# Softmax subtraction and scaling and the experts' low parts on GpSimd behind the first block, outputs added in three chunks

## The chip, the cores and the metric

The kernel runs on one core of a Trainium2 chip. The metric is the device time of one execution in microseconds; the time before is 1141.91 us, the median of 3 runs (1141.68 to 1142.55).

Engine names follow the profile: PE is TensorE (PEld its weight loads), DVE is VectorE, ACT is ScalarE, POOL is GpSimd, SP is SyncE, whose queue issues the DMAs of this kernel.

## The reference

4096 rows (2 x 2048) of 512 features go through a latent attention and then through a gated expert layer whose weights are quantised to three values. Each branch is normalised on its way in and on its way out and added to the row.

```python
Q = (h @ Wq.T + bq).reshape(b, t, H, HD).transpose(0, 2, 1, 3)      # H=16 heads, HD=32
V = (h @ Wv.T + bv).reshape(b, t, H, HD).transpose(0, 2, 1, 3)
attn_logits = einsum('bhtd,lhd->bhtl', Q, latent) / sqrt(HD)         # L=64 latents
topk_logits, topk_idx = top_k(attn_logits, 4)
weights = softmax(topk_logits)
weighted = einsum('bhtk,bhtkd->bhtd', weights, selected latents)
attn = (weighted + V).transpose(0, 2, 1, 3).reshape(b, t, d) @ Wo.T + bo
...
wu, wg, wd = ternary_quant(W_up), ternary_quant(W_gate), ternary_quant(W_down)
hidden = silu(x @ wu.T) * (x @ wg.T)                                 # 2048 wide
ffn = hidden @ wd.T
...
x = x + layernorm(attn(layernorm(x)))
x = x + layernorm(ffn(layernorm(x)))
```

## The kernel before, in words

The rows are cut into 8 blocks b of 512 rows, each of four tiles t of 128 rows. The expert layer of a block runs in 16 steps e, one for each 128 of the 2048 hidden features. While the experts of block b run, the attention of block b + 1 is spread over the same steps, and some of block b + 2's input normalisation. The order of all instructions on every engine and queue is the order in which the program writes them; each engine works through its own queue in that order, and a waiting instruction holds what is behind it. The synchronisation itself is made by the tile framework.

One step of the experts (the loop over e at the end of the kernel): eight matmuls into the up product `pu`; `tanh` on ScalarE; `silu` on VectorE (L728); eight matmuls into the gate product `pg`; `gate` on VectorE (L733), which makes `h`; `high` on ScalarE (L744), which rounds `h` to fp32r as `hi`; `low` (L749), which makes `lo = h - hi`; and in the next step `down` (L759), where TensorE multiplies `hi` and `lo` (as weights) with a piece of the down matrix into the accumulators `acc` of the four tiles. The down projection of step e - 1 comes behind the gate matmuls of step e; that of step 15 is in step 0 of the next block. [...]

Between these pieces the step has four slots, called by `do(k)`: slot 3 ahead of `tanh`, slot 0 behind it, slot 1 behind the gate matmuls, and slot 2 behind `down`. The function `pieces` says which piece of the next block's attention is put in which slot of which step. For the attention of a block, i runs from 0 to 7 over pairs of heads:

- `q(c)`: query matmuls (L353) and the copy `qT` with bias on ScalarE (L358); `l(c)`: logits (L367) and their copy `w` on ScalarE, for i = 2c and 2c + 1
- `m(i)`: the 8 largest of each 64 (L385); `r(i)`: eight match_replace (L393) that mark the four taken, then `w - best` (L395) and `top - best` (L397), all on VectorE
- `e(i)`: the exponentials of `top` (L402) and of `w` (L403) on ScalarE
- `n(i)`: sum and reciprocal of the four, the masking of `w` (L410), and its scaling by the reciprocal (L413), on VectorE
- `z(i)`: a transpose within blocks on VectorE (L420), a DMA of the result to DRAM (`dz`, L425) and four DMAs back (`wT`, L428), which complete the transpose
- `v(c)` and `y(c)`: value matmuls (L440), and on top of them the matmuls of the weights `wT(2c)` and `wT(2c+1)` with the latents (L457); `attnT` is the copy on ScalarE
- `o(t)`, `o_bias`, `o_rstd`, `o_apply_scalar`: output projection, bias and normalisation; `o_apply_scalar` adds the row on GpSimd (L502); then `f_stats` to `f_split`, the normalisation and transposed hi/lo halves that the experts of the next block read

Block 0 has an attention of its own ahead of all, in the order of a written list (`FIRST_STEPS`), and block 1's attention, a `FirstAttention` as well, runs in block 0's steps. In the steps of blocks 1 to 6 the attentions of blocks 2 to 7 run; block 7 has experts alone. `pieces` puts m(i) in slot 0 of step 1 + i (slot 1 for i = 0), r(i) in slot 2 of step 1 + i, n(i) and z(i) in slot 1 of step 2 + i, e(i) in slot 3 of step 2 + i; q(2) and q(3) in slot 0 of steps 3 and 5; and for c = 0 and 1 v(c), y(c) and l(c + 2) in slot 0 of step 4 + 2c, for c = 2 and 3 v(c) and y(c) in slot 1 of that step. o(t) are in step 10, the additions of L502 in step 11.

The experts' output of block b is finished in the steps of block b + 1: the last `down`, statistics and reciprocal root in step 0, and `y_out` for the four tiles in step 1, which normalises on VectorE (L276), adds the row on GpSimd (L810) and stores it (L812, on SP). In block 7 the four are spread over steps 1 and 2.

Of the kernel before, what the change touches and what calls it, by code (L numbers as in the profile page):

```python
# [10 lines left out]
F32 = mybir.dt.float32  # L11
# [3 lines left out]
ALU = mybir.AluOpType  # L15
AX = mybir.AxisListType

P = 128
H = 16
HD = 32  # L20
L = 64
# [37 lines left out]
def latent_attention_ternary_glu(  # L59
# [15 lines left out]
    nc = tc.nc  # L75
# [6 lines left out]
    NB = NT // TB  # L82
    G = 2 * TT
# [39 lines left out]
    for n, i in RAW_ORDER:  # L123
        raw[n, i] = wpool.tile([P, CH], F32, tag="chunk", name=f"raw_{n}_{i}", bufs=6 * DC)
# [21 lines left out]
    def load_up(n, src, pieces):  # L146
        for i in pieces:
            k, h = halves[i]
            nc.sync.dma_start(
                out=raw[n, i], in_=src[k * P : (k + 1) * P, h * CH : (h + 1) * CH]  # L150
            )
# [88 lines left out]
    class Norm:  # L240
        def __init__(self, name):
            self.name = name
            self.mv = small.tile([P, TT, 2], F32, tag="mv", name=f"mv_{name}")
            self.rs = small.tile([P, TT], F32, tag="rs", name=f"rs_{name}")
            self.nm = None
# [34 lines left out]
    def row(name):  # L280
        return work.tile([P, D], F32, tag="row", name=name, bufs=4)
# [9 lines left out]
    class Attention:  # L291
        def __init__(self, b):
            self.b = b
            self.hT = None
            self.attnT = None
            self.norm_a = Norm(f"a{b}")
            self.norm_o = Norm(f"o{b}")
            self.norm_f = Norm(f"f{b}")
            self.rows = {}
            self.qT, self.w, self.top, self.m8, self.left, self.wT, self.pv = ({} for _ in range(7))  # L300
            self.po = {}
            self.far = {}
# [85 lines left out]
        def r(self, i):  # L388
            w, m8 = self.w[i], self.m8.pop(i)
            left = work.tile([P, G, L], F32, tag="left", name=f"left_{self.b}_{i}", bufs=2)  # L390
            self.left[i] = left
            for g in range(G):
                nc.vector.match_replace(left[:, g, :], m8[:, g, :], w[:, g, :], TAKEN)  # L393
            best = m8[:, :, 0:1]
            nc.vector.tensor_tensor(w, w, best.to_broadcast([P, G, L]), ALU.subtract)  # L395
            self.top[i] = small.tile([P, G, K_TOP], F32, tag="top", name=f"top_{self.b}_{i}", bufs=2)
            nc.vector.tensor_tensor(  # L397
                self.top[i], m8[:, :, 0:K_TOP], best.to_broadcast([P, G, K_TOP]), ALU.subtract
            )
# [5 lines left out]
        def n(self, i):  # L405
            w = self.w[i]
            ri = small.tile([P, G], F32, tag="ri", name=f"ri_{self.b}_{i}", bufs=2)
            nc.vector.tensor_reduce(ri, self.top.pop(i), AX.X, ALU.add)
            nc.vector.reciprocal(ri, ri)
            nc.vector.scalar_tensor_tensor(  # L410
                w, self.left.pop(i), TAKEN, w, ALU.is_equal, ALU.mult
            )
            nc.vector.tensor_tensor(  # L413
                w, w, ri.rearrange("p (g o) -> p g o", o=1).to_broadcast([P, G, L]), ALU.mult
            )

# [123 lines left out]
    class FirstAttention(Attention):  # L540
# [111 lines left out]
        def b_low(self):  # L652
            low = row("bias_low")
            nc.vector.tensor_tensor(low, bo_sb, self.bias.bitcast(F32), ALU.subtract)
            nc.vector.tensor_scalar(low, low, ident[:, 1:2], 0.0, ALU.mult, ALU.add)
            nc.vector.scalar_tensor_tensor(
                self.bias, self.bias.bitcast(F32), ident[:, 0:1], low, ALU.mult, ALU.add
            )
# [43 lines left out]
    class Experts:  # L702
# [43 lines left out]

        def low(self, e):
            lo = self.part("lo", e)
            nc.vector.tensor_tensor(lo, self.h.pop(e), self.hid[e][0].bitcast(F32), ALU.subtract)  # L749
            self.hid[e].append(lo)  # L750

        def down(self, e, tiles=range(TT), last=True):
# [46 lines left out]
            r = self.b * TB + t * P  # L799
            nc.sync.dma_start(out=out[r : r + P, part], in_=x[:, part])  # L800

        def y_out(self, t, engine=nc.gpsimd):
            x = x_tiles[self.b][t]
            if self.b == NB - 2:
                y = self.y[t]
                self.norm.apply(y, y, t)
            else:
                y = row(f"y_{self.b}_{t}")
                self.norm.apply(y, self.acc[t], t)
            engine.tensor_tensor(x, x, y, ALU.add)  # L810
            r = self.b * TB + t * P
            nc.sync.dma_start(out=out[r : r + P, :], in_=x)  # L812

# [3 lines left out]
    A = FirstAttention(0)  # L817
# [119 lines left out]
    def pieces(A, after):  # L937

        at = {(e, k): [] for e in range(EC) for k in range(4)}

        def put(e, k, f, *args):
            at[e, k].append(lambda: f(*args))

        if A.b > 1:
            put(0, 2, A.q, 0)
            put(1, 1, A.q, 1)
            put(3, 0, A.q, 2)
            put(5, 0, A.q, 3)
        put(1, 0, A.l, 0)
        put(2, 0, A.l, 1)  # L950
        for i in range(8):
            put(1 + i, 0 if i else 1, A.m, i)
            put(1 + i, 2, A.r, i)
            put(2 + i, 3, A.e, i)
            put(2 + i, 1, A.n, i)
            put(2 + i, 1, A.z, i)
        for c in range(2):
            if A.b > 1:
                put(4 + 2 * c, 0, A.v, c, gate_psum)
                put(4 + 2 * c, 0, A.y, c)  # L960
            put(4 + 2 * c, 0, A.l, c + 2)
            if A.b == 1:

                put(4 + 2 * c, 2 - c, A.v, c)
                put(4 + 2 * c, 2 - c, A.y, c)
        for c in range(2, DC):
            put(4 + 2 * c, 1, A.v, c)
            put(4 + 2 * c, 1, A.y, c)

        if after is not None and after.b == 2:  # L970
            for t in range(TT):
                put(10, 2, after.a_stats, t)
            put(10, 2, after.a_rstd, 0, TT)
        elif after is not None:
            put(9, 2, after.a_stats, 0)
            put(9, 2, after.a_stats, 1)
            put(10, 0, after.a_stats, 2)
            put(10, 0, after.a_stats, 3)
            put(10, 0, after.a_rstd, 0, TT)
            for t in range(TT):  # L980
                put(10, 1, after.a_apply, t)
            for t in range(TT):
                put(10, 2, after.a_blocks, t)
        put(10, 2, A.o, 0, range(DC), gate_psum)
        put(10, 2, A.o_bias, 0)
        for t in range(1, TT):
            if after is not None and after.b == 2:
                for i in (t - 1,) if t < 3 else (2, 3):
                    put(10, 2, after.a_apply, i)
                    put(10, 2, after.a_blocks, i)  # L990
            put(10, 2, A.o, t)
            put(10, 2, A.o_bias, t)
        put(10, 2, A.o_rstd, 0, 2)
        put(10, 2, A.o_rstd, 2, 4)
        for t in range(TT):
            put(11, t // 2, A.norm_o.shift, t)
            put(11, t // 2, A.o_apply_scalar, t)
        put(11, 2, A.f_stats, 0)
        put(11, 2, A.f_stats, 1)
        put(11, 2, A.f_rstd, 0, 2)  # L1000
        put(12, 0, A.f_stats, 2)
        put(12, 0, A.f_stats, 3)
        put(12, 0, A.f_rstd, 2, 4)
        for t in range(TT):
            put(12, 1 + t // 2, A.norm_f.shift, t)
            put(12, 1 + t // 2, A.f_apply_scalar, t)
        put(12, 2, A.f_blocks, 0)
        put(12, 2, A.f_blocks, 1)
        put(13, 0, A.f_blocks, 2)
        put(13, 0, A.f_blocks, 3)  # L1010
        put(13, 0, A.f_load, 0)
        put(13, 1, A.f_load, 1)
        for t in range(TT):
            put(14 + t // 2, 2 - t // 2, A.f_split, t)
        if after is not None:
            put(15, 2, after.a_load)
        return at

    prev = None
    for b in range(NB):  # L1020
        if b > 0:
            A, nxt = nxt, after
        after = None
        F = Experts(b, A.split())
        at = {}
        for e in range(EC):
# [25 lines left out]
            F.silu(e)  # L1052
            if e == 1 and 0 < b < NB - 1:
                for t in range(TT):
                    prev.y_out(t)
            F.up("g", e)
            do(1)
            F.gate(e)
            F.high(e)
            if e == EC - 1 and b == NB - 1:  # L1060

                nc.scalar.activation(columns[:, 11:12], columns[:, 10:11], AF.Sqrt)
# [12 lines left out]
            if e == 0 and prev is not None:  # L1075
# [2 lines left out]
                        prev.y_copy(t)  # L1078
                    prev.y_stats(t)
                prev.y_rstd(0, TT)  # L1080
            if e > 0 or b < NB - 1:
                F.low(e)
            if b == NB - 1 and e in (1, 2):
                prev.y_out(2 * e - 2)
                prev.y_out(2 * e - 1)
        prev = F


# [77 lines left out]
```

## Time and profile before

| what | us |
|---|---|
| median of 3 runs | 1141.91 |
| span of the profiled execution | 1140.3 |
| one block of 1 to 6 (831.02 / 6) | 138.5 |
| TensorE busy in such a block | 138.35 |
| VectorE busy in block 2 | 104.73 |
| GpSimd busy in block 2 | 17.50 |
| ScalarE busy in block 2 | 43.45 |

The profile gives the execution's span from its first to its last instruction; the runs' time has some 1.6 us more. In the profile's lines an instruction is named by its engine, its line in the code, its operation and out<-in with the program's tile names; x8 stands for eight instructions. A row of costly groups ends with their busy time and the mean nanoseconds of one, and, behind a second bar, the idle time of the engine just ahead of them with what ended it. A line of the order of time begins with its start and its duration in us from the span's start. A row of a stretch has its length, then busy time and (x instructions) of PE, PEld, DVE, ACT and POOL, the granted clock, and the share and rate of the DMAs. SPq is the queue that issues DMAs: the duration there is that of the issue, and the page's last part gives the time from issue to landing.

### The profile page before, as it was taken

The numbers are of one execution on the slowest core, as the hardware profiler recorded it, in microseconds if no ns is written. First come the engines' busy times: TensorE is split into PE (matmuls) and PEld (weight loads), VectorE is DVE, ScalarE is ACT, GpSimd is POOL, SyncE is SP. The second block draws the span as 40 slices with busy tenths as digits, with TensorE's granted clock in tenths as the row PEclk, the third lists the DMA queues.
The fourth block names the chain that finished last, engine by engine and source line by source line (L and its number), as shares of the span: only waits on it lengthen the run. The fifth ranks groups of instructions, "written<-read, shape, count | busy, mean of one in ns | idle before, by whom it ended". The sixth has DMA issues, their size and how long they took to land.

```text
span 1140.3 us, 14487 instructions
## 1 busy us (share of the span) xinstructions
PE 1127.9 (99%) x4602; PEld 771.9 (68%) x4602; DVE 836.3 (73%) x2952; ACT 411.9 (36%) x714; POOL 163.5 (14%) x203
## 2 busy tenths in 40 slices
PE   9999999999999999999999999999999999999997
PEld 5547666767667675776657766586675866758886
DVE  6978968687866887678877778678786787847435
ACT  4985642332233332333214333153321433224223
POOL 1057003110032000320002200022001120021200
PEclk9999999999999999999999999999999999999999
DMA  9800221432213322222222222232321412102000
GB/s 350 305 0 20 74 93 38 111 120 84 82 52 98 102 86 81 72 77 93 93 74 75 83 93 95 63 99 66 112 75 56 111 65 93 61 5 74 37 1 37
DMA packets 98428, 97.16 MB, mean 85 GB/s; under 512 B 8368, under 2 KB 70832, under 8 KB 98352
## 3 DMA queue, kind: packets, MB, share of 16 engines
q1 hardware_dynamic: 98352, 96.24, 26.8%
q8 instruction: 36, 0.59, 0.2%
q14 instruction: 40, 0.33, 0.1%
HBM read 59.51 MB, written 36.70 MB: 84 GB/s over the span
## 4 chain that ended last, share of the span: by engine, by line
PE 89%; DVE 5%; DMA 4%; ACT 1%; issue 0%; SPq 0%; ACTq 0%; DVEq 0%
PE pg L716 20%; PE pu L716 19%; PE acc L759 19%; PE po L468 8%; PE pv L440 8%; PE pq L353 7%; PE pv L457 2%; PE pl L367 2%; DMA raw_d<-in_wdT 1%; DVE left L393 1%; DMA raw_g<-in_wgT 1%; DMA wv<-in_wvT 1%; DVE m L385 1%; DMA raw_u<-in_wuT 1%; PE pq L577 1%; DMA hT<-far_a 1%
## 5 line engine op out<-in xcount | busy, mean ns | idle before, releaser
L716 PE MATMUL pg<-hT_f,tern_g 128*128 128x512 f32 x512 | 207.8, 406 | 0.0
L716 PE MATMUL pu<-hT_f,tern_u 128*128 128x512 f32 x512 | 204.8, 401 | 0.0
L759 PE MATMUL acc<-tern_d,hi 128*128 128x512 f32 x512 | 203.6, 398 | 0.0
L759 PE MATMUL acc<-tern_d,lo 128*128 128x512 f32 x512 | 200.0, 391 | 1.0 <-DVE lo L749 0.9
L716 PE MATMUL pg<-lT_f,tern_g 128*128 128x512 f32 x512 | 199.8, 390 | 0.0
L716 PE MATMUL pu<-lT_f,tern_u 128*128 128x512 f32 x512 | 199.1, 390 | 0.0
L725 ACT ACTIVATE h<-pu,columns 128x512 f32<-128x512 f32 x128 | 87.1, 680 | 202.8 <-PE pu L716 202.8
L728 DVE SCALAR_TENSOR_TENSOR h<-h,pu 128x512 f32<-128x512 f32 x128 | 85.9, 671 | 93.5 <-ACT h L725 93.5
L744 ACT CAST hi<-h 128x512 fp32r<-128x512 f32 x128 | 79.1, 618 | 199.2 <-DVE h L733 199.1
L733 DVE TENSOR_TENSOR h<-h,pg 128x512 f32<-128x512 f32 x128 | 86.5, 675 | 63.4 <-PE pg L716 62.3
L759 PEld LDWEIGHTS acc<-tern_d,hi 128*128 128x128 f32 x512 | 96.2, 188 | 32.8 <-issue 13.6
L716 PEld LDWEIGHTS pg<-hT_f,tern_g 128*128 128x128 f32 x512 | 96.2, 188 | 25.3 <-issue 1.4
L716 PEld LDWEIGHTS pu<-hT_f,tern_u 128*128 128x128 f32 x512 | 96.1, 188 | 25.1 <-issue 3.1
L759 PEld LDWEIGHTS acc<-tern_d,lo 128*128 128x128 f32 x512 | 96.2, 188 | 22.9 <-DVE lo L749 2.2
L716 PEld LDWEIGHTS pu<-lT_f,tern_u 128*128 128x128 f32 x512 | 96.2, 188 | 22.5 <-issue 3.1
L716 PEld LDWEIGHTS pg<-lT_f,tern_g 128*128 128x128 f32 x512 | 96.3, 188 | 21.5 <-issue 2.9
L749 DVE TENSOR_TENSOR lo<-h,hi 128x512 fp32r<-128x512 f32 x128 | 89.9, 702 | 23.1 <-ACT hi L744 23.1
L440 PE MATMUL pv<-hT,wv 128*128 128x512 f32 x224 | 100.8, 593 | 0.3 <-ACT w L375 0.3
L393 DVE MATCH_REPLACE8 left<-m,w 128x64 f32<-128x64 f32 x512 | 100.3, 209 | 0.0
L468 PE MATMUL po<-wo,attnT 128*128 128x512 f32 x224 | 97.3, 592 | 0.0
L353 PE MATMUL pq<-hT,wq 128*128 128x512 f32 x192 | 86.7, 595 | 0.9 <-DMA hT<-far_a 0.6
L468 PEld LDWEIGHTS po<-wo,attnT 128*128 128x128 f32 x224 | 42.6, 190 | 50.7 <-issue 48.3
(140 smaller groups left out, 1312.0 us busy)
## 6 DMA issues: line engine op xcount, KB each, us to landing
dz<-z SPq DMA_DIRECT2D x56, 256.0 KB, 2.0
wT<-dz SPq DMA_DIRECT2D x224, 64.0 KB, 1.9
x<-in_x SPq DMA_DIRECT2D x32, 256.0 KB, 3.7
out_x<-x SPq DMA_DIRECT2D x32, 256.0 KB, 2.0
far_f<-zf SPq DMA_DIRECT2D x28, 256.0 KB, 2.8
hw<-far_f SPq DMA_DIRECT2D x56, 128.0 KB, 3.5
xa<-in_x SPq DMA_DIRECT2D x6, 1024.0 KB, 5.3
far_a<-za SPq DMA_DIRECT2D x24, 256.0 KB, 2.9
```

The source lines that it names most:

```text
L353: nc.tensor.matmul(pq, lhsT=wq[:, k, c * P : (c + 1) * P], rhs=self.taken(k), start=(k == 0), stop=(k == DC - 1),)
L367: nc.tensor.matmul(pls[pr][:, t * P : (t + 1) * P], lhsT=qT[rows, t * P : (t + 1) * P], rhs=lk[rows, c, :], start=True, stop=True, tile_po ...
L393: nc.vector.match_replace(left[:, g, :], m8[:, g, :], w[:, g, :], TAKEN)
L440: nc.tensor.matmul(self.pv[c], lhsT=wv[:, k, c * P : (c + 1) * P], rhs=self.ordered(k), start=(k == 0), stop=False,)
L468: nc.tensor.matmul(self.po[t], lhsT=self.attnT[:, c, t * P : (t + 1) * P], rhs=wo[:, c, :], start=(c == 0), stop=(c == DC - 1),)
L716: nc.tensor.matmul(p, lhsT=tern[n, 2 * k + e // 8][:, (e % 8) * P : (e % 8 + 1) * P], rhs=self.parts[i][:, k], start=(k, i) == pairs[0], s ...
L725: nc.scalar.activation(self.h[e], self.pu[e], AF.Tanh, scale=half_u[0])
L728: nc.vector.scalar_tensor_tensor(self.h[e], self.h[e], 1.0, self.pu.pop(e), ALU.add, ALU.mult)
L733: nc.vector.tensor_tensor(self.h[e], self.h[e], self.pg.pop(e), ALU.mult)
L744: nc.scalar.copy(hi, self.h[e])
L749: nc.vector.tensor_tensor(lo, self.h.pop(e), self.hid[e][0].bitcast(F32), ALU.subtract)
L759: nc.tensor.matmul(self.acc[t], lhsT=part[:, t * P : (t + 1) * P], rhs=wd, start=(e == 0 and i == 0), stop=(e == EC - 1 and i == 1),)
```

## The change

In blocks above 1 the attention's subtraction of the largest value (L395) and its scaling (L413) go to GpSimd (`aside`). In the steps of blocks 1 to 6 the experts' `low` goes to GpSimd, and its place in the program from behind slot 2 to directly behind `high`; in the first and the last block it stays on VectorE. For the attentions that run in blocks 1 to 6, e(i) goes from slot 3 to slot 0 and is put first of the three lists (behind q), z(i) from slot 1 to slot 2; r(i) is now behind z of the step. `y_out` is split: `y_apply` normalises all four tiles in step 1 as before, and `y_add` adds and stores tile 0 in step 1, tiles 1 and 2 in step 2 and tile 3 in step 3, each behind the step's `low`.

```diff
+            self.aside = nc.gpsimd if b > 1 else nc.vector
...
-            nc.vector.tensor_tensor(w, w, best.to_broadcast([P, G, L]), ALU.subtract)
+            self.aside.tensor_tensor(w, w, best.to_broadcast([P, G, L]), ALU.subtract)
...
-            nc.vector.tensor_tensor(
+            self.aside.tensor_tensor(
                 w, w, ri.rearrange("p (g o) -> p g o", o=1).to_broadcast([P, G, L]), ALU.mult
             )
...
         def low(self, e):
             lo = self.part("lo", e)
-            nc.vector.tensor_tensor(lo, self.h.pop(e), self.hid[e][0].bitcast(F32), ALU.subtract)
+            engine = nc.gpsimd if 0 < self.b < NB - 1 else nc.vector
+            engine.tensor_tensor(lo, self.h.pop(e), self.hid[e][0].bitcast(F32), ALU.subtract)
             self.hid[e].append(lo)
...
-        def y_out(self, t, engine=nc.gpsimd):
+        def y_apply(self, t):
+            if self.b < NB - 2:
+                self.y = getattr(self, "y", {})
+                self.y[t] = row(f"y_{self.b}_{t}")
+                self.norm.apply(self.y[t], self.acc[t], t)
+            else:
+                self.norm.apply(self.y[t], self.y[t], t)
+
+        def y_add(self, t):
             x = x_tiles[self.b][t]
...
-            engine.tensor_tensor(x, x, y, ALU.add)
+            nc.gpsimd.tensor_tensor(x, x, self.y[t], ALU.add)
             r = self.b * TB + t * P
             nc.sync.dma_start(out=out[r : r + P, :], in_=x)
...
+        for i in range(8):
+            put(2 + i, 0 if A.b > 1 else 3, A.e, i)
         put(1, 0, A.l, 0)
         put(2, 0, A.l, 1)
         for i in range(8):
             put(1 + i, 0 if i else 1, A.m, i)
+            put(2 + i, 1, A.n, i)
+            put(2 + i, 2 if A.b > 1 else 1, A.z, i)
             put(1 + i, 2, A.r, i)
-            put(2 + i, 3, A.e, i)
-            put(2 + i, 1, A.n, i)
-            put(2 + i, 1, A.z, i)
...
             if e == 1 and 0 < b < NB - 1:
                 for t in range(TT):
-                    prev.y_out(t)
+                    prev.y_apply(t)
             F.up("g", e)
             do(1)
             F.gate(e)
             F.high(e)
+            if 0 < b < NB - 1:
+                F.low(e)
+            if e in (1, 2, 3) and 0 < b < NB - 1:
+                for t in ((0,), (1, 2), (3,))[e - 1]:
+                    prev.y_add(t)
...
-            if e > 0 or b < NB - 1:
+            if b == 0 or b == NB - 1 and e > 0:
                 F.low(e)
             if b == NB - 1 and e in (1, 2):
-                prev.y_out(2 * e - 2)
-                prev.y_out(2 * e - 1)
+                for t in (2 * e - 2, 2 * e - 1):
+                    prev.y_apply(t)
+                    prev.y_add(t)
```

More of the change, by code (lines that the diff above doesn't have):

```diff
@@ L800, in z_out @@
             nc.sync.dma_start(out=out[r : r + P, part], in_=x[:, part])
-        def y_out(self, t, engine=nc.gpsimd):
-            x = x_tiles[self.b][t]
[L804 to L810, printed above, removed]
+        def y_apply(self, t):
[6 more added lines that the diff above has]
+        def y_add(self, t):
+            x = x_tiles[self.b][t]
+            nc.gpsimd.tensor_tensor(x, x, self.y[t], ALU.add)
             r = self.b * TB + t * P
```

## The prediction

> **What bounds the kernel now.** I read the page's busy times first, then the stretches of blocks 1 to 6 (the only ones in which the change alters anything that runs in a repeating step), then the order of time in one of them, block 2, which begins at 351.52 and whose steps are called e here.
>
> ```profile
> span 1140.3 us, 14487 instructions
> ...
> PE 1127.9 (99%) x4602; PEld 771.9 (68%) x4602; DVE 836.3 (73%) x2952; ACT 411.9 (36%) x714; POOL 163.5 (14%) x203
> ```
> ```profile
> 351.52:490.08 138.56, 138.32 (x561) 94.50 (x560) 104.73 (x368) 43.45 (x77) 17.50 (x21) 1.00 0.28 84
> ...
> sum 831.02, PE 830.08 PEld 566.97 DVE 621.14 ACT 260.54 POOL 103.84; mean PE 138.35 PEld 94.49 DVE 103.52 ACT 43.42 POOL 17.31
> ```
>
> TensorE is busy all the time, at a granted clock of 1.00. In the six blocks 831.02 us pass and TensorE is busy 830.08: 0.94 us is all that any relief of VectorE can win there. What counts is therefore the other direction: each of TensorE's operands arrives with a margin, and a change that moves an arrival past its margin costs the difference, since nothing later gives it back.
>
> **What moves.** Per block VectorE loses 8 subtractions, 8 scalings and 16 low parts; GpSimd gets them.
>
> ```profile
> L395 DVE TENSOR_TENSOR w<-w,m 128x512 f32<-128x512 f32 x64 | 44.9, 702 | 2.3
> L413 DVE TENSOR_TENSOR w<-w,ri 128x512 f32<-128x512 f32 x64 | 44.7, 698 | 2.2
> ...
> L810 POOL TENSOR_TENSOR x<-x,y 128x512 f32<-128x512 f32 x28 | 35.5, 1298 | 25.7 <-DVE y L276 25.7
> ```
>
> On VectorE that is 8 x 1.40 + 16 x 0.70 = 22.4 us off 104.7. GpSimd has run none of the three operations, so they are bounded: below by VectorE's 0.70, above by 1.75, the longest record of GpSimd's 128x512 additions at L502. I take 1.28, the median record of L810's, because they have the same size and two SBUF operands; four of them in a row take 4.98, so 1.24 from start to start. That adds 32 x 1.28 = 41 us to 17.5, or 58 of 138.5: no engine is filled. Most of the work is covered. A low part in a common step ends about 0.69 (gate) + 0.62 (high part) + 1.28 + 0.1 = 2.7 us after the gate product starts, and the down projection that reads it comes behind three groups of eight matmuls (down of the step before, up and gate of the next), 3 x 1.81 = 5.4 us. If that cover were gone, a low part would cost 0.6 us. The subtraction only has to be ready for the exponential of the next step. The four y_apply stay in e = 1. Three places are not covered.
>
> **Place one, wT(1) in e = 4.** These lines of the order of time show the matmuls of L457, which need the transposed softmax weights wT(0) and wT(1), and the DMAs that bring wT(1).
>
> ```profile
> 384.59 0.34 SPq L425 DMA_DIRECT2D dz<-z  x1
> 386.63 1.73 SPq L428 DMA_DIRECT2D wT<-dz  x4
> ```
> ```profile
> 384.72 0.39 PE L716 MATMUL pg<-lT_f,tern_g 128*128 128x512 f32 x1
> ...
> 392.10 1.08 PE L457 MATMUL pv<-wT,lv 128*64 128x512 f32 x4
> ```
>
> From dz's issue to the last landing of wT is 2.04 (to the first wT issue) + 1.30 (to the fourth) + 1.9 (its median landing) = 5.24 us, so wT(1) is there at 389.83 and waits 2.27 us for TensorE. Both halves of L457 start together, so 392.10 is the due time.
>
> The change does three things to that DMA. The transpose z(1) goes from slot 1 of e = 3 to slot 2, behind the gate product. The exponential goes from slot 3 to slot 0, where qT(2) is copied ahead of it on ScalarE. And in e = 3 the last of the four row additions, with its store, is put ahead of z(1)'s DMAs: SP takes its queue in order, so dz(1) waits behind a store that waits for GpSimd. In numbers:
>
> - the query copy starts at 383.32 (ScalarE, 0.69), the two exponentials behind it end at 384.66 (starts 0.13 apart, 0.61 the second), the masking L410 on VectorE 384.70 to 385.34 (0.64);
> - gate product: its matmuls end at 385.11 (0.39 after 384.72), VectorE is free at about 385.3; 0.69 makes 385.98; the high part 0.62 makes 386.62;
> - GpSimd: scaling(1) from 385.43, next start 386.67; low(3) 386.70, addition(3) 387.95, ended 389.23;
> - SP: store of row 3 at 389.26, dz(1) 0.39 behind it at 389.65 (z(1) itself is ready at about 387.5). That is 5.06 later than 384.59; wT(1) lands at 389.65 + 5.24 = 394.89.
>
> TensorE stands from 392.10 to 394.9: 2.8 us. By the bounds of the new operations' price (the addition is known): at 0.70 the low part is done 0.57 sooner and 2.25 us remain; at 1.75 it starts at 387.18, after the scaling, and is done 0.98 later, 3.8 us.
>
> **Place two, wT(3) in e = 6.** No row is stored in e = 5, but the query copy and the order of z are the same:
>
> ```profile
> 404.16 0.34 SPq L425 DMA_DIRECT2D dz<-z  x1
> 406.26 1.73 SPq L428 DMA_DIRECT2D wT<-dz  x4
> ```
> ```profile
> 412.18 1.08 PE L457 MATMUL pv<-wT,lv 128*64 128x512 f32 x4
> ```
>
> Copy from 403.40, exponentials to 404.74, masking to 405.42, scaling 405.51 to 406.79, z(3) to 407.56 (0.71), dz(3) at 407.6, landed 412.83: 0.65 us late. With 0.70 for the scaling 0.1, with 1.75 1.1. For wT(5) and wT(7) there is no query copy ahead, and the same steps give 0.3 and 0.7 us later; their margins are 1.15 (dz at 424.25, due 430.64) and 1.5 (439.46, 446.18).
>
> **Place three, low(11) in e = 11.** GpSimd adds four rows of the attention branch there (L502) and the code puts low(11) behind all four.
>
> ```profile
> 466.43 5.50 POOL L502 TENSOR_TENSOR x<-x,o 128x512 f32<-128x512 f32 x4 [0.31 <-ACT o L271]
> ```
> ```profile
> 469.83 0.94 DVE L749 TENSOR_TENSOR lo<-h,hi 128x512 fp32r<-128x512 f32 x1
> ...
> 471.95 0.39 PE L759 MATMUL acc<-tern_d,hi 128*128 128x512 f32 x1
> ```
>
> Without VectorE's low part between them the additions end at 466.43 + 4 x 1.25 = 471.4; low(11) is there at 472.7, and with 0.07 for the semaphore its weight load, due at 471.95, is 0.8 us late. At 0.70 for the low part it is 0.2, at 1.75 1.3. What is queued behind low(11) on GpSimd is the reciprocal root of the next normalisation (rs_f), 0.6 us later than before; its rows have margin until the next block's first matmul, which itself shifts.
>
> **Sum.** 2.8 + 0.65 + 0.8 = 4.25 us a block, six blocks, 25.5 us. The first and the last block keep their engines and their order. The profiled execution has a span of 1140.3; the median of the runs is 1141.91, 1.6 more, and I keep that distance: 1140.3 + 25.5 + 1.6 = 1167.4, say 1167. The bounds of GpSimd's price give (2.25 + 0.1 + 0.2) x 6 = 15, so 1157, and (3.8 + 1.1 + 1.3) x 6 = 37, so 1179.
>
> [...] Low(11) in the line above took 0.94 against 0.70 alone while a GpSimd addition ran, and the addition after it 1.75 against 1.29: both engines lose when they overlap with two SBUF operands each. [...]
>
> **Rivals.** (a) GpSimd is dear: broadcast operands, or the rounding to fp32r, which no GpSimd row shows, at 1.75 or beyond. For it: nothing measured; against it: L810's records lie close together (1.26 at the least, 1.28 the median). 1179 and more. Chance 0.12.
> (b) Only SP's order bites, at the first place; z(3) and low(11) arrive just in time. 2.8 x 6 = 17: 1159; with the cheap bound 2.25 x 6 = 13.5: 1155. For it: places two and three are small, 0.65 and 0.8, and each is a difference of some ten durations. Against it: both come out late with every price from 0.70 on. Chance 0.2.
> (c) Not slower: SP lets dz(1) go in time. It decides at 392.10 - 5.24 = 386.86: if dz(1) leaves by then, and dz(3) by 406.94, TensorE never stands, GpSimd's work is all covered and the 0.94 us of idle is the most to win: 1141 to 1142. For it: VectorE is freed, which is late with the gate product by 4.5 us in e = 8 (matmuls ended at 427.27, product from 431.81). Against it: z(1) cannot start before the gate product, 385.1 at the earliest, and the store is written ahead of it. Chance 0.1.
> The forecast itself has 0.58.
>
> **How the numbers follow.** Of no change are times within 0.2%, some 2.3 us, about what a measurement of this kernel can tell. Rival (c) cannot pass that by the 0.94 us; I leave 0.03 for faster, for a cause that I don't see, 0.07 for the same, and 0.90 for slower. The range goes from 1150, under (b)'s 1155 by 0.8 us a block for a margin that I read too small, to 1180, the dear bound; it leaves out (c) and the far end of (a).
>
> **What would show it.** In the profile after: a wait of TensorE at L457 for DMA wT, some 12 times, of 2 to 3 and of half a us in turn; SP's dz in e = 3 directly behind a store; in e = 11 a wait of L759 for a GpSimd low part; TensorE's busy time unchanged near 1128. GpSimd's rows for the three operations give the price. If dz(1) leaves ahead of the store, or wT lands before 392, I am wrong about the main term; if the margins of low parts elsewhere fail, a place is missing and the time is above 1180.

## The result and the profile after

| | before | after |
|---|---|---|
| median of the runs, us | 1142.23 (1141.68 to 1143.35) | 1176.09 (1173.13 to 1180.14) |
| span of the profiled execution, us | 1140.3 | 1174.2 |
| blocks 1 to 6, us | 831.02 | 865.38 |
| TensorE busy in them, us | 830.08 | 847.36 |
| VectorE busy in block 2, us | 104.73 | 85.96 |
| GpSimd busy in block 2, us | 17.50 | 53.60 |

The changed kernel is slower by 2.9%: ratio 1.0293, interval 1.0270 to 1.0316, some 34 us. All of it lies in blocks 1 to 6 (865.38 - 831.02 = 34.36). Line numbers are higher by one to four behind the edits: L457 is now L458, L425 is L426, L428 is L429, L413 is L414, L749 is L751, L759 is L761, L810 is L814, L812 is L816.

The page of the changed kernel, its span and busy times:

```profile
span 1174.2 us, 14537 instructions
...
PE 1144.2 (97%) x4602; PEld 775.7 (66%) x4602; DVE 725.4 (62%) x2760; ACT 411.9 (35%) x714; POOL 380.1 (32%) x395
```

The stretches of blocks 1 to 6, of which block 2 is shown, and their sum:

```profile
357.78:501.13 143.35, 140.54 (x561) 94.71 (x560) 85.96 (x336) 43.49 (x77) 53.60 (x53) 1.00 0.27 81
...
sum 865.38, PE 847.36 PEld 571.56 DVE 510.96 ACT 260.62 POOL 319.03; mean PE 141.23 PEld 95.26 DVE 85.16 ACT 43.44 POOL 53.17
```

VectorE is relieved as meant and TensorE waits. Only 17.1 of the 34.36 us show as its idle time: before, 0.94 us of the six blocks were idle, now 865.38 - 847.36 = 18.02. The other half hides in "busy" records, so I measured from start to start: the time from one step's first up matmul to that of the next step. The waits of TensorE (total us, times, longest):

```profile
PE pv L458 <- DMA wT<-dz: 14.4, 6, 2.7
PE acc L761 <- POOL lo L751: 2.6, 6, 0.4
```

Place one, in block 2. The first up matmul of step e = 4, from which the issue of dz(1) is counted, in the kernel before and in the changed one:

```profile
386.76 0.39 PE L716 MATMUL pu<-hT_f,tern_u 128*128 128x512 f32 x1
```
```profile
392.96 0.39 PE L717 MATMUL pu<-hT_f,tern_u 128*128 128x512 f32 x1
```

GpSimd's order of time in e = 3 of the changed kernel:

```profile
391.66 1.05 POOL L414 TENSOR_TENSOR w<-w,ri 128x512 f32<-128x512 f32 x1 [3.00 <-DVE w L411]
392.97 1.29 POOL L751 TENSOR_TENSOR lo<-h,hi 128x512 fp32r<-128x512 f32 x1 [0.27 <-ACT hi L745]
394.22 1.28 POOL L814 TENSOR_TENSOR x<-x,y 128x512 f32<-128x512 f32 x1
```

SP's queue behind it, with the store of row 3 and dz(1):

```profile
395.53 0.36 SPq L816 DMA_DIRECT2D out_x<-x  x1
395.98 0.38 SPq L426 DMA_DIRECT2D dz<-z  x1
```

TensorE's L458 in e = 4:

```profile
398.30 1.07 PE L458 MATMUL pv<-wT,lv 128*64 128x512 f32 x2
...
401.57 1.07 PE L458 MATMUL pv<-wT,lv 128*64 128x512 f32 x2 [2.20 <-DMA wT<-dz]
```

Scaling, low part, row addition, store, and only then dz(1): 3.02 us behind the start of e = 4, where before it was 2.17 ahead (384.59 against 386.76). L458 has its first two matmuls on time, with wT(0); those for wT(1) start 3.27 later (1.07 of it is the first two's run, 2.20 idle); before, all four began together. Place two is one group, wT(3) in e = 6, which needs 1.89 instead of 1.08:

```profile
421.65 1.89 PE L458 MATMUL pv<-wT,lv 128*64 128x512 f32 x4
```

Place three, GpSimd in e = 11 of the same block: the four additions, and low(11) behind them; then the matmul of e = 12 that waits for it.

```profile
476.71 5.05 POOL L503 TENSOR_TENSOR x<-x,o 128x512 f32<-128x512 f32 x4 [0.66 <-ACT o L271]
481.70 1.29 POOL L751 TENSOR_TENSOR lo<-h,hi 128x512 fp32r<-128x512 f32 x1
```
```profile
483.05 0.50 PE L761 MATMUL acc<-tern_d,lo 128*128 128x512 f32 x1 [0.43 <-POOL lo L751]
```

From start to start over the six blocks, place one (e = 4) costs 25.4 us (3.3 to 5.3 a block), place two (e = 6) 4.5, place three (e = 12) 4.4; less than 0.1 us lies beside them.

### The profile page after: what moved, and what is told of

The parts are those of the page before. It is cut to its first block, busy times and chain, and to the rows that moved or that the text cites. A ratio compares the mean times of both kernels' runs of the same rounds, so it can differ in the third digit from the quotient of the medians.

```text
span 1174.2 us, 14537 instructions
## 1 busy us (share of the span) xinstructions
PE 1144.2 (97%) x4602; PEld 775.7 (66%) x4602; DVE 725.4 (62%) x2760; ACT 411.9 (35%) x714; POOL 380.1 (32%) x395
## 4 chain that ended last, share of the span: by engine, by line
PE 77%; DMA 7%; DVE 6%; POOL 4%; issue 3%; ACT 2%; SPq 1%; POOLq 0%; ACTq 0%; DVEq 0%
PE pg L717 17%; PE acc L761 16%; PE pu L717 16%; PE po L469 8%; PE pq L354 7%; PE pv L441 6%; PE pv L458 3%; PE pl L368 3%; POOL x L503 2%; DMA dz<-z 1%; DMA hT<-far_a 1%; DMA wT<-dz 1%; DMA raw_d<-in_wdT 1%; DVE left L394 1%; DMA raw_g<-in_wgT 1%
## 5 line engine op out<-in xcount | busy, mean ns | idle before, releaser
L751 POOL TENSOR_TENSOR lo<-h,hi 128x512 fp32r<-128x512 f32 x96 | 123.8, 1289 | 323.2 <-ACT hi L745 323.2
L761 PE MATMUL acc<-tern_d,lo 128*128 128x512 f32 x512 | 200.6, 392 | 3.6 <-POOL lo L751 2.6
L761 PE MATMUL acc<-tern_d,hi 128*128 128x512 f32 x512 | 203.5, 397 | 0.0
L729 DVE SCALAR_TENSOR_TENSOR h<-h,pu 128x512 f32<-128x512 f32 x128 | 86.3, 674 | 152.1 <-ACT h L726 152.1
L761 PEld LDWEIGHTS acc<-tern_d,hi 128*128 128x128 f32 x512 | 96.1, 188 | 32.8 <-issue 13.6
L761 PEld LDWEIGHTS acc<-tern_d,lo 128*128 128x128 f32 x512 | 96.1, 188 | 28.1 <-POOL lo L751 5.1
L414 POOL TENSOR_TENSOR w<-w,ri 128x512 f32<-128x512 f32 x48 | 50.2, 1045 | 116.6 <-DVE w L411 116.6
```

Of the source, the lines that this page charges most:

```text
L414: self.aside.tensor_tensor(w, w, ri.rearrange("p (g o) -> p g o", o=1).to_broadcast([P, G, L]), ALU.mult)
L729: nc.vector.scalar_tensor_tensor(self.h[e], self.h[e], 1.0, self.pu.pop(e), ALU.add, ALU.mult)
L751: engine.tensor_tensor(lo, self.h.pop(e), self.hid[e][0].bitcast(F32), ALU.subtract)
L761: nc.tensor.matmul(self.acc[t], lhsT=part[:, t * P : (t + 1) * P], rhs=wd, start=(e == 0 and i == 0), stop=(e == EC - 1 and i == 1),)
```

## The experiments

All compute the whole reference. Theory A is that of the prediction: late operands, by the order of the queues, above all the store ahead of dz(1). Theory B is that GpSimd itself is dear, so that the loss goes with its work and not with the order. Theory C is that moving z behind the gate product is the loss by itself. The ratio is to the kernel before, run on the same chip. The table gives what the trace of block 2 shows: when SP issues dz(1), counted from the first up matmul of e = 4, and by how much the steps e = 4, 6 and 12 (places one, two, three) are longer than before (11.20, 11.20 and 5.44 us from start to start). The kernels with one chunk alone, with chunks alone and with q(0) later stand only in their own sections; the trace of one chunk alone is from an execution at a granted clock of 0.948.

| kernel | dz(1) | e = 4 | e = 6 | e = 12 | median, us | kernel before, us |
|---|---|---|---|---|---|---|
| before | -2.17 | 0 | 0 | 0 | | |
| after | +3.02 | 3.26 | 0.81 | 0.75 | 1176.09 | 1142.23 |
| stores late | +0.50 | 0.58 | 0.74 | 0.75 | 1154.52 | 1141.23 |
| two rows in e = 3 | +4.23 | 4.64 | 0.67 | 0.73 | 1187.14 | 1141.23 |
| new order, all on VectorE | +1.97 | 2.00 | 2.09 | 0.83 | 1198.89 | 1141.23 |
| one chunk, low(11) on VectorE | +0.51 | 0.53 | 0.83 | 0 | 1151.51 | 1142.14 |
| one chunk, exponentials first | -0.28 | 0 | 0 | 0.73 | 1147.17 | 1142.14 |
| all three repairs | -0.28 | 0 | 0 | 0 | 1142.54 | 1142.14 |
| low parts alone | -2.08 | 0 | 0 | 0.74 | 1145.87 | 1141.61 |
| softmax alone | +0.51 | 0.47 | 0.72 | 0 | 1150.70 | 1141.61 |

### Is it the row's addition and store in e = 3?

Two ways to take them away from dz(1). The first adds all four rows in e = 1 again, behind `y_apply`:

```diff
                 for t in range(TT):
                     prev.y_apply(t)
+                    prev.y_add(t)
...
-            if e in (1, 2, 3) and 0 < b < NB - 1:
-                for t in ((0,), (1, 2), (3,))[e - 1]:
-                    prev.y_add(t)
```

> The change, with all four row additions and stores back in step 1 (one chunk). Theory A (the store of row 3 stands ahead of dz(1) on SP, and low(3) and the addition ahead of the store on GpSimd): in step 3 dz(1) leaves when z(1) is done; in the changed kernel's profile that is some 2.5 us sooner, so the wait of L458 in step 4 falls from 3.3 to about 0.5 us, the stretches of half clock behind it vanish, places two (0.8) and three (0.6) stay: 6 x 1.9 = 11 us over the kernel before, 1151 to 1155. [...] Theory C (moving z behind the gate product is the loss): 1168 to 1176.

Measured 1155.66 (ratio 1.0155, interval 1.0099 to 1.0211). The interval is wide because the profiled execution took 1169.45 at a granted clock of 0.948, and the other three 1155.18 to 1155.88 at 0.999. The median is just above the range of A, which ended at 1155, and far below that of C and the 1176.09 of the change, which theory B leaves as it is.

The second leaves the additions on GpSimd where the change put them and moves only the stores on SP, behind z's DMAs:

```diff
             do(2)
+            if e in (1, 2, 3) and 0 < b < NB - 1:
+                for t in ((0,), (1, 2), (3,))[e - 1]:
+                    prev.y_store(t)
```

> The change, with the three chunks of additions where they are on GpSimd, but the stores of the rows written behind slot 2 of their step, so behind dz and wT of z. It separates SP's queue from GpSimd's. If the store on SP is the cause: as with one chunk, 1151 to 1156, with the GpSimd order unchanged (low, addition, subtraction). If GpSimd's queue is the cause: 1172 to 1176.

Measured 1154.52 (1.0117, 1.0102 to 1.0132). SP's queue in e = 3 of block 2, with dz(1) now ahead of the store:

```profile
389.52 0.33 SPq L426 DMA_DIRECT2D dz<-z  x1
391.56 1.76 SPq L429 DMA_DIRECT2D wT<-dz  x4
393.41 0.38 SPq L818 DMA_DIRECT2D out_x<-x  x1
```

The order of DMA issues on one queue is worth 20.6 us (a loss of 13.3 in place of 33.9, each against its own runs of the kernel before), with GpSimd's work untouched. The wait of L458 for wT falls out of the list, and place one keeps 0.58.

### Does it grow with the queue ahead of dz(1)?

Two rows are added and stored in e = 3 instead of one:

```diff
-                for t in ((0,), (1, 2), (3,))[e - 1]:
+                for t in ((0,), (1,), (2, 3))[e - 1]:
```

> The change with rows 2 and 3 added and stored in step 3 (chunks of 1, 1, 2): it doubles the suspected cost. Theory A: dz(1) leaves one GpSimd addition later, 1.25 us, so the wait of L458 in step 4 grows from 3.3 to about 4.5 us: 6 x 1.25 = 7.5 us more, and with longer waits more stretches of half clock (1.0 to 1.7 us each, 3 in the profile of the change, up to 6 here): 1183 to 1190. Theory B and C: the same work on the same engines, 1174 to 1178.

Measured 1187.14 (1.0400, 1.0383 to 1.0418). In block 2 the SP queue:

```profile
396.53 1.58 SPq L816 DMA_DIRECT2D out_x<-x  x2
398.20 0.38 SPq L426 DMA_DIRECT2D dz<-z  x1
```

And the second half of L458:

```profile
403.96 1.07 PE L458 MATMUL pv<-wT,lv 128*64 128x512 f32 x2 [3.58 <-DMA wT<-dz]
```

One more addition puts dz(1) 1.21 later (+4.23 against +3.02) and e = 4 of this block 1.38 longer, and the loss 12 us larger (45.9 against 33.9). 1.38 in each of six blocks would be 8.3; the other blocks lose more, since five of the six run at half the clock behind the wait (last section), where in the changed kernel it was three.

### Is it GpSimd, or the order alone?

Rival (a) says that GpSimd is dear. Here the three operations are on VectorE again, in the change's order and with its chunks:

```diff
-            self.aside = nc.gpsimd if b > 1 else nc.vector
+            self.aside = nc.vector
...
-            engine = nc.gpsimd if 0 < self.b < NB - 1 else nc.vector
+            engine = nc.vector
```

> The change with subtraction, scaling and low parts on VectorE, at the changed places in the order; only order and chunks are left of the change. Theory A: low(3) now keeps VectorE from z(1), and scaling keeps it from the gate product; z(1) is done about 4.1 us later than before and its last wT lands 1.9 us late; wT(3) the same, wT(5) and wT(7) about 0.5 late each: 1142 + 6 x 4.7 = 1170, 1162 to 1172. Theory B (GpSimd as such): nothing runs on GpSimd that did not before, so 1141 to 1146.

Measured 1198.89 (1.0503, 1.0488 to 1.0519): more than the change, and more than A reckoned. B falls, and A is wrong in size. TensorE's waits:

```profile
PE pv L458 <- DMA wT<-dz: 20.3, 18, 2.0
PE pu L717 <- DVE h L729: 6.1, 12, 0.7
```

VectorE's order of time in e = 3 of block 2:

```profile
394.14 0.68 DVE L734 TENSOR_TENSOR h<-h,pg 128x512 f32<-128x512 f32 x1
395.51 0.69 DVE L751 TENSOR_TENSOR lo<-h,hi 128x512 fp32r<-128x512 f32 x1 [0.69 <-ACT hi L745]
396.12 0.71 DVE L421 STREAM_TRANSPOSE z<-w 128x512 f32<-128x512 f32 x1
```

The low part is written ahead of z, so VectorE stands for the high part, and z stands behind it: gate product, high part, low part and transpose in a row put dz(1) at +1.97 although the row was stored long before. This is so in every step, so wT(3) and wT(5) are late too: 2.1 and 2.2 us in e = 6 and 8, and the silu (L729), behind all this, makes the up product of the next step wait in two steps a block (the 0.83 of e = 12 is one of them). The three wT places give (2.0 + 2.1 + 2.2) x 6 = 38 of the 58 us by block 2. By all six blocks they give 42.8, the steps e = 12 to 14 another 9.7, and e = 10 5.7, whose wait I did not take apart. With this order GpSimd is what keeps the low part out of z's way. It is not the cause of the loss.

### The other two places, one repair each

With one chunk some 0.5 us are left at place one in each block, 0.7 at place two and 0.7 at place three. First low(11) goes to VectorE at its old place, behind slot 2 (and one chunk):

```diff
+            engine = nc.gpsimd if 0 < self.b < NB - 1 and e != 11 else nc.vector
...
+            if b == 0 or b == NB - 1 and e > 0 or e == 11 and b < NB - 1:
                 F.low(e)
```

> One chunk as before, and in step 11 the low part back on VectorE behind slot 2. Theory A: the wait at place three goes, 0.6 to 0.75 us a block, so 3.6 to 4.5 us less than with one chunk alone (1155.5): 1151 to 1152; no wait of L761 for a GpSimd low part is left in the trace. If place three is covered by something else that is late there: 1154 to 1156.

Measured 1151.51 (1.0084, 1.0068 to 1.0100); no wait of L761 for a GpSimd low part is left. Then, in its stead, the exponentials are put ahead of the query copies in the slot lists, so that masking, scaling and z don't wait for the copies of q(2) and q(3):

```diff
+        for i in range(8):
+            put(2 + i, 0 if A.b > 1 else 3, A.e, i)
         if A.b > 1:
...
             put(5, 0, A.q, 3)
-        for i in range(8):
-            put(2 + i, 0 if A.b > 1 else 3, A.e, i)
```

> One chunk as before, and the exponentials ahead of the query copy in slot 0 of steps 3 and 5, the rest as changed. Theory A: masking and scaling of i = 1 and 3 come 0.5 to 1.2 us earlier, z then starts right behind the gate product, and wT(1) and wT(3) land in time; 0.5 + 0.75 us a block, 7.5 us less than with one chunk alone: 1147 to 1149. Theory C (z behind the gate product is the loss by itself): place two stays at 0.7, 1152 to 1155.

Measured 1147.17 (1.0045, 1.0031 to 1.0059): dz(1) and dz(3) leave 0.78 sooner, and places one and two are gone. z is still behind the gate product here, so theory C falls as well. All three repairs together:

> All three undone together: one chunk, exponentials ahead of the query copy, low part of step 11 on VectorE; subtraction, scaling and the other low parts stay on GpSimd, z stays behind the gate product. Theory A: nothing is late any more: 1141 to 1144, the time of before, with VectorE at some 87 us of busy time a block against 104.7. If GpSimd's work costs anything by itself: above 1146.

Measured 1142.54 over 11 runs, the kernel before 1142.14 (1.0007, 0.9998 to 1.0016). Its page:

```profile
span 1140.4 us, 14537 instructions
...
PE 1127.3 (99%) x4602; PEld 770.6 (68%) x4602; DVE 720.1 (63%) x2766; ACT 410.0 (36%) x714; POOL 375.7 (33%) x389
```

SP's issues of dz(1) and dz(3) in block 2:

```profile
386.49 0.34 SPq L426 DMA_DIRECT2D dz<-z  x1
...
406.58 0.34 SPq L426 DMA_DIRECT2D dz<-z  x1
```

TensorE's L458 in e = 4 and e = 6 of that block:

```profile
392.11 1.08 PE L458 MATMUL pv<-wT,lv 128*64 128x512 f32 x4
...
412.19 1.08 PE L458 MATMUL pv<-wT,lv 128*64 128x512 f32 x4
```

116 us of VectorE's work are gone (836.3 to 720.1) and GpSimd has 212 more, and the time is that of before: TensorE was the bound and is again.

### The parts alone, on the kernel before

Three chunks alone (`y_out` split as in the change, nothing else):

> The kernel before with the three chunks alone, its order otherwise kept. Theory A: z(1) stands ahead of the store there (slot 1), so the store delays no DMA that is due: 1140.5 to 1142, the same as before. If later row additions and stores cost anything by themselves (a later load of the next rows, GpSimd's queue): 1143 to 1150.

Measured 1141.85 over 10 runs against 1142.14 (0.9997, 0.9987 to 1.0006). Without the moved low part and z, dz(1) leaves at -2.16, ahead of the store.

The low parts alone, on GpSimd directly behind `high`:

> The kernel before with the low parts alone on GpSimd, directly behind the high part. Theory A: only place three is left: 0.6 to 0.75 us a block, 3.6 to 4.5 us over before: 1145 to 1147. [...]

Measured 1145.87 (1.0038, 1.0025 to 1.0052). Its one new wait is that of place three:

```profile
PE acc L760 <- POOL lo L750: 2.6, 6, 0.4
```

The softmax part alone (subtraction and scaling on GpSimd, e, z and r moved; low parts on VectorE at the old place, one chunk):

> Subtraction and scaling on GpSimd with the moved exponentials and z, the low parts back on VectorE behind slot 2, one chunk. Theory A: the rest of place one (0.5) and place two (0.75), 7.5 us over before, place three none: 1148 to 1151. Together with the low parts alone and the chunks alone this leaves the rest of the change's 34 us to the three being together: the store in step 3 behind a late addition.

Measured 1150.70 (1.0084, 1.0070 to 1.0097). The parts add up to -0.3 + 4.3 + 9.1 = 13 us, which is about what the one-chunk kernel loses (14.4). The change loses 34. The other 20 come only when the store of row 3 and the moved z and low part meet. No run has the store and the moved z without the low part, so how much of the 20 the low part adds is not shown.

### A version that beats both?

What TensorE still waits for at a block's begin is hT for q(0) (0.4 in the repaired kernel). On top of the three repairs, q(0) and l(0) go a step later:

```diff
         if A.b > 1:
-            put(0, 2, A.q, 0)
+            put(1, 0, A.q, 0)
+            put(1, 1, A.l, 0)
             put(1, 1, A.q, 1)
```

> A try for less than both: all three undone, and the block's first query matmuls one slot later (behind the up product of step 1), since TensorE waits 0.2 to 0.5 us for hT there in each block. If hT is in time then and the logits come out early enough in step 1: 1.8 us less than with all three, 1139.5 to 1141. If the gate product of step 1 is late then: 1142 to 1146.

Measured 1144.36 over 8 runs (1.0026, 1.0016 to 1.0037): the time is that of the second branch but the wait is another. The query matmuls q(1), now directly behind l(0), wait for ScalarE to copy its logits out:

```profile
PE pq L354 <- ACT w L376: 4.1, 6, 0.7
```

No version that I ran beats the kernel before.

## Why the prediction was right, and where its size was off

**The bound.** That TensorE has nothing to win is shown by the repaired kernel (1142.54 against 1142.14), and that each lateness adds up in full by the table: the longer steps e = 4, 6 and 12 of block 2, times six, give 12.4 of the 13.3 us of the kernel with late stores, 4.4 of 5.0 with the exponentials first, 4.4 of 4.3 with low parts alone.

**Place one** was right in its mechanism. The working said scaling, low(3), addition and store in this order, and dz(1) 5.06 later than before; it is 5.19 later (from -2.17 to +3.02). The size was off: the term of 2.8 us is 3.3 to 3.7 as a plain wait (3.43 on the mean of blocks 2, 3 and 6). The trip from dz's issue to the last wT was taken at 5.24, from a step in which nothing else was in SP's queue; behind a store just issued it is 5.5 to 5.9. That is 0.6 x 6 = 3.8 us.

**Half the clock** was not in the sum at all. The forecast took every matmul's duration from before. Directly behind the wait at place one, the granted clock is 0.50 for 3.41 us in blocks 1, 4 and 5, and 1.00 in blocks 2, 3 and 6. The step e = 4 is 4.87, 5.29 and 4.89 us longer than before in the first three, and 3.26, 3.74 and 3.31 in the others. The idle time ahead of L458 is alike in pairs: 2.28 and 2.30 in blocks 1 and 5 and 2.20 and 2.27 in 2 and 6, 2.67 in block 4 and 2.68 in 3. So a stretch of half clock costs some 1.6 us, and three of them 4.7. Together: 25.5 + 3.8 + 4.7 + 0.6 (place two) - 0.4 (place three) is 34.2 of the 34.4.

**The range** held partly by luck. Its upper end of 1180 stood for a GpSimd price of 1.75 us, which did not come; what put the time 9 us above the forecast, the longer trip and the half clock, had no term in it. One of the four runs took 1180.14.

**Place two**, forecast at 0.65, is 0.68 to 0.90 a block, and **place three**, forecast at 0.8, some 0.74. The 0.07 reckoned from the low part's end to the work that reads it is 0.06 in the trace of the change (482.99 to 483.05 in block 2). The exponentials and low(11), put back one at a time, take each away; that the query copy is what delays wT(3) is shown by the first. The margins of wT(5) and wT(7) hold, as said: dz is 0.06 and 0.40 later there, and step 8 takes 10.11 us as before.

**GpSimd's price** was taken at 1.28 for all three operations. The three lines in the trace of the changed kernel, with the count, the least, median and longest duration in ns, and the first and last start:

```profile
L751 POOL TENSOR_TENSOR lo<-h,hi x96: 1266/1290/1302, 218.2 to 1078.9; 128x512 fp32r<-128x512 f32 x96
...
L396 POOL TENSOR_TENSOR w<-w,m x48: 1049/1060/1072, 234.7 to 1021.8; 128x512 f32<-128x512 f32 x48
...
L414 POOL TENSOR_TENSOR w<-w,ri x48: 1042/1046/1050, 237.2 to 1025.5; 128x512 f32<-128x512 f32 x48
```

The low part is right: with fp32r output it takes 1.29, the row additions without it 1.28. The two with a broadcast operand are cheaper, 1.05, so rival (a) is out by the rows as well as by the runs.

**Signs named ahead.** 12 waits of L458 were announced; the list has six, since place two's wait lies inside a group of four matmuls (1.89 for 1.08). TensorE's busy time was to stay near 1128 and is 1144.2: a record of a matmul that waits (1.89 for 1.08), or runs at half the clock (3.41 of 3.41 us busy from 257.74), counts as busy. That sign was wrong.

**Rival (b)**, SP's order alone, falls: places two and three exist. **Rival (c)** named the points from which it decides, dz(1) by 386.86 and dz(3) by 406.94. The repaired kernel, whose block 2 begins 0.14 later than that of before, has them at 386.49 and 406.58 and isn't slower. It is the case that a different order would have made true.

## What to carry to other kernels

Here TensorE was busy for 830.08 of 831.02 us, and taking 116 us off VectorE gained nothing (1142.54 against 1142.14). With an engine as full as that, the price of a move is the margin of every operand behind it: work out its new issue time through each queue in order, with the stores that share the queue, and compare with the time at which the consumer needs it. Parts that are harmless alone (chunks 0 us) can cost most of the loss together (20 of 34 us here), so look for where their instructions meet in one queue. Measure a loss from start to start: half of this one (17.3 of 34.4 us) stood in busy time.

## What the runs showed of the hardware

**The clock fell to half behind three of six waits, and the length of the wait does not tell which.** In the changed kernel TensorE's idle time at place one is 2.28, 2.67 and 2.30 us in blocks 1, 4 and 5, where the granted clock falls to 0.50 behind it, and 2.20, 2.68 and 2.27 in blocks 2, 3 and 6, where it stays at 1.00. The drops begin at 257.74, 691.23 and 834.59 and last 3.41 us each. Their starts are 433.49 and 143.36 us apart; 433.49 / 127 and 143.36 / 42 both give 3.413, about the length of a drop. My estimate from these starts and lengths is that they fall on a grid of that spacing. Laid on that grid, the windows at the wait of place one in blocks 1 to 5, in order of time (length, then busy time of PE, PEld, DVE, ACT, POOL, and the granted clock third from the end):

```profile
254.33:257.74 3.41, 1.13 (x3) 0.19 (x2) 0.00 (x0) 0.00 (x0) 0.12 (x1) 1.00 0.68 196
257.74:261.15 3.41, 3.41 (x20) 2.94 (x20) 0.00 (x0) 1.77 (x3) 0.00 (x0) 0.50 0.54 189
...
397.69:401.10 3.41, 1.69 (x4) 0.19 (x2) 0.50 (x1) 0.00 (x0) 1.04 (x1) 1.00 0.31 83
401.10:404.51 3.41, 2.94 (x22) 1.87 (x23) 0.00 (x0) 1.43 (x3) 0.00 (x0) 1.00 0.96 301
...
544.46:547.87 3.41, 1.95 (x18) 1.16 (x18) 0.00 (x0) 0.69 (x1) 0.00 (x0) 1.00 0.85 225
...
687.82:691.23 3.41, 1.57 (x12) 0.79 (x14) 0.00 (x0) 0.49 (x1) 0.00 (x0) 1.00 0.80 228
...
831.18:834.59 3.41, 1.11 (x3) 0.19 (x2) 0.00 (x0) 0.00 (x0) 0.75 (x1) 1.00 0.42 127
```

A window with 1.11, 1.13 or 1.57 us of TensorE's work is followed by one at half the clock (the second line, in block 1); one with 1.69, 1.95 or, in block 6, 2.10 is not. These runs show no single border between the two: with two rows in e = 3, windows of block 2 with 1.60 and 1.64 are not followed by a drop, and windows already at half the clock with 1.92 and 2.22 are followed by another at half. So the wait at place one costs 3.3 to 3.7 us in the blocks without a drop and 4.9 to 5.3 in those with one, and the runs of the changed kernel spread with the clock: 1173.13 at a mean granted clock of 0.998, 1176.0 and 1176.17 at 0.995, 1180.14 at 0.990. With two rows in e = 3, where the wait is longer (3.58 us idle in block 2), five of the six blocks have such a stretch, and two of those last two windows.

**A subtraction on VectorE beside an addition on GpSimd.** A subtraction of 128x32 on VectorE, 0.18 to 0.19 us elsewhere, takes 0.65 when it starts in the middle of a GpSimd row addition (394.22 to 395.50 above), and the addition is not longer for it:

```profile
394.89 0.65 DVE L398 TENSOR_TENSOR top<-m 128x32 f32<-128x32 f32 x1
```

It ends 0.04 behind the addition. The same instruction in e = 2, which starts 0.17 behind the start of an addition (385.12 to 386.41), takes 1.17 and ends 0.05 behind it; all six blocks show both. The working has both engines losing, and in the kernel before they did: low(11) took 0.94 and the addition beside it 1.75. In these two cases of the changed kernel VectorE alone loses. Here it costs nothing on TensorE's path: no step outside the three places is longer by more than 0.1 us on the sum of the six blocks.
